# A two-layer graph attention kernel: sets of seven matrix products run into each other, the second product runs one graph later, and score rows are spread by GpSimd

## The chip, the cores and the metric

The kernel runs on one core of one Trainium2 chip. A core has five engines with their own instruction queues: TensorE (PE in the profile; its weight loads are listed apart as PEld), VectorE (DVE), ScalarE (ACT), GpSimd (POOL) and SyncE (SP, which here only issues transfers). TensorE writes to PSUM, which VectorE and ScalarE read. Sixteen DMA engines move data between HBM and the core's SBUF. The metric is the device time of one execution in microseconds (us).

## What is computed

The input is x of shape (32, 512, 512) in float32, that is 32 graphs of 512 nodes with 512 features, and a 0/1 matrix adj of shape (32, 512, 512) in int32. Each graph goes through a layer norm with ReLU, two layers of graph attention and a residual sum:

```python
def gat_layer(x, mask, W, a_src, a_dst, bias, concat):
    xl = (x @ W).reshape(B, N, H, F)
    asrc = jnp.einsum('bnhf,hf->bnh', xl, a_src)
    adst = jnp.einsum('bnhf,hf->bnh', xl, a_dst)
    e = jax.nn.leaky_relu(asrc[:, :, None, :] + adst[:, None, :, :], 0.2)
    e = jnp.where(mask[..., None], e, NEG_INF)
    attn = jax.nn.softmax(e, axis=1)
    out = jnp.einsum('bsdh,bshf->bdhf', attn, xl)
    ...
h = jnp.maximum(_layernorm(x, axis=-1), 0.0)
mask = (adj > 0) | jnp.eye(N, dtype=bool)[None]
h1 = jax.nn.elu(gat_layer(h, mask, W1, att_src1, att_dst1, b1, concat=True))
out = x + gat_layer(h1, mask, W2, att_src2, att_dst2, b2, concat=False)
```

The first layer has H = 4 heads of F = 256 features, the second one head of 512. So a graph needs four large products: x by W1 ("project1"), attention by features for four heads ("gather1"), h1 by W2 ("project2") and attention by features again ("gather2").

## The kernel before

**Products in sets of seven.** Each large product of 2 x 2 blocks is done with seven block products instead of eight (Strassen's scheme in Winograd's form). `sevens` (L866) does project1, project2 and gather2; `gather1` (L1079) does the heads' products in pairs. The sums of blocks that feed the seven products are VectorE subtractions (`sums` L823, `sums1` L1016, `sums2` L1225). Three running sums, named "a", "b" and "g" in `ACC` (L864), each hold one double bank of PSUM; product 1 is copied from a's bank to g's (the `COPY2` of `mm` into `mm` on ScalarE), and after each product its bank is emptied to SBUF by ScalarE (`act` with Copy) or VectorE (subtract or add). PSUM has four double banks, handed out by `Banks` (L45). `LAST` (L907) gives the order of the seven: 1, 5, 6, 3, 7, 2, 4; `PAIRS_OF` (L1070) gives 1, 5, 6, 2, 7, 3, 4 for gather1. Each set is run to its end before the next begins.

**Attention weights.** `Soft` (L657) makes the attention weights of one head. `columns` (L691) takes the node scores and spreads the row of source scores to all 128 partitions; `first` (L710) makes each target's maximum and sum over 128 x 512 blocks: leaky ReLU on ScalarE (`l<-as,z`), masked minimum on VectorE (`l<-l,mt`), exponential on ScalarE (`l<-l,low`). Its results form a row that is spread too (`rr`); `second` (L763) builds the weights `p` from that row: four VectorE sums (`p<-rr,z`), two transfers by GpSimd that add the mask from HBM to p (`accumulate`, L430, `p<-dm`), and four exponentials on ScalarE (`p<-p,z`). `spread` (L665) brings a row to all partitions: a VectorE transpose, a small transfer to HBM (`das`, `drr`), and a transfer that reads it back once for each partition (`as<-das`, `rr<-drr`, 512 KB).

**Other parts.** `masks` (L555) turns adj into a bf16 mask `m`, writes it to HBM (`dm`) and transposes it by DMA (`mt`). `norm` (L586) makes the layer norm's statistics, with the root as a power on GpSimd (L597); `norm_turn` (L606) normalises on ScalarE and turns x by a DMA transpose (`x<-adj`) between two ScalarE copies (`adj<-x`, `ht<-x`). `elu` (L983) finishes the first layer.

**What sets the order.** The program is not emitted as it is written. Every instruction is added to a `Program` (L87) with its engine, a planned cost and the keys it reads and writes. TensorE's order is the written one; for ScalarE, VectorE, GpSimd and SP a planner (`order`, L234) simulates the run from the planned costs and picks an order, which each engine then follows strictly. Transfers are planned with a fixed lead, a size and a tail (L97). The steady loop (L1371) handles at step i: gather1 of graph i+1 (two pairs), project1 of graph i+2 (two halves), the second layer's softmax and gather2 of graph i, and project2 of graph i+1.

Of the kernel before, what the change touches and what calls it, by code (L numbers as in the profile page):

```python
# [44 lines left out]
class Banks:  # L45


    def __init__(self, tiles):
        self.tiles = tiles
        self.free = [(i, j) for i in range(len(tiles)) for j in range(2)]  # L50
        self.written = {q: 512 for q in self.free}

    def take(self, width=512, seeded=0):
        n = [sum(i == k for k, _ in self.free) for i in range(len(self.tiles))]
        fit = [q for q in self.free if self.written[q] >= seeded]
        half = next((q for q in fit if n[q[0]] == 1), fit[0])
        least = min(self.written[q] for q in fit)
# [15 lines left out]
    def take2(self, width, seeded=0):  # L73
        whole = [i for i, j in self.free if j == 0 and (i, 1) in self.free]
        least = {i: min(self.written[i, j] for j in range(2)) for i in whole}
        i = min((i for i in whole if least[i] >= seeded), key=least.get)
        self.free = [q for q in self.free if q[0] != i]
        for j in range(2):
            self.written[i, j] = max(width, self.written[i, j] if seeded else 0)
        return [("mm", i, j) for j in range(2)], self.tiles[i]  # L80
# [218 lines left out]
def tile_gat(  # L299
# [66 lines left out]
    half = sbuf.tile([P, NT], F32, name="half")  # L366
    nc.vector.memset(half, -0.5)
# [11 lines left out]
    xl2 = sbuf.tile([P, NT, DO + 2], F32, name="xl2")  # L379
# [7 lines left out]
    xrs = slots("xr", 4, [P, N])  # L387
    ls = slots("l", 3, [P, N])
    ps_ = slots("p", 3, [P, NT, N])
    m = sbuf.tile([P, NT, N], BF16, name="m")  # L390
# [5 lines left out]
    drs = slots("drr", 2, [2 * NT, P], F32, dram)  # L396
    mds = slots("dm", 3, [P, NT, N], BF16, dram)
    stats = slots("stats", 2, [P, NT, nc.vector.BN_STATS_DIM + nc.vector.BN_AGGR_DIM + 1])
    zs = slots("z", 4, [P, 5, 2, NT])
# [13 lines left out]
    )  # L413

# [140 lines left out]
    def masks(b):  # L555

        for t in range(NT):
            ak, a = adjs.take()
            dma(0.75, (), [ak], a, adj[b, t * P : (t + 1) * P, :])
            dve(  # L560
                0.34, [ak], [("m", t)], nc.vector.tensor_scalar,
                m[:, t, :], a, 0.0, -BIG, op0=OP.is_le, op1=OP.mult,
            )
            adjs.give(ak)
        blocks = bass.AP(tensor=m.tensor, offset=m.offset, ap=[m.ap[0], [N + P, NT], [1, P]])
        every = [("m", t) for t in range(NT)]
        dve(
            0.5, every, every, nc.vector.tensor_max,
            blocks, blocks, diag[:, None, :].to_broadcast([P, NT, P]),
        )  # L570
        MASK[b] = mk, md = mds.take()
        dma(0.45, every, [mk], md.rearrange("p t n -> p (t n)"), m.rearrange("p t n -> p (t n)"))
        tk, mt = mts.take()

        for t in (0, 2):
            prog.add(
                "SP", 1.3, every, [tk + (t // 2,)],
                lambda t=t: nc.sync.dma_start_transpose(
                    mt[:, t : t + 2].rearrange("p t d r -> p (t d) r"),
                    m[:, t : t + 2].rearrange("p t n -> p (t n)"),  # L580
# [5 lines left out]
    def norm(b):  # L586
        sk, st = stats.take()
        S, A = nc.vector.BN_STATS_DIM, nc.vector.BN_AGGR_DIM
        for t, (xk, xt) in enumerate(XT[b]):
# [4 lines left out]
        dve(TINY, every, every, nc.vector.tensor_scalar_add, rstd, st[:, :, S + 1], EPS)  # L594
        prog.add(
            "POOL", 1.0, every, every,
            lambda: nc.gpsimd.tensor_tensor(rstd, rstd, half, op=OP.pow),  # L597
        )
# [58 lines left out]
    class Soft:  # L657
# [7 lines left out]
        def spread(self, v, keys, rows, to, through, n=NT):  # L665

            k = rows * n
            ok, o = to.take()
            dk, dr = through.take()

            c = 32 // k
            sb = o[:, 0, :32]
            dve(
                0.12, keys, [ok], nc.vector.transpose,
                sb, bass.AP(tensor=v.tensor, offset=v.offset, ap=[v.ap[0], [1, k], [0, c]]),
            )
            dma(
                0.03, [ok], [dk], dr[:k].rearrange("k (b j) -> b k j", j=32),
                bass.AP(
                    tensor=sb.tensor, offset=sb.offset, ap=[[c * sb.ap[0][0], P // c], [1, 32]]  # L680
                ),
                0.55,
            )
            dma(
                0.18 * rows * n, [dk], [ok], o[:, :rows, : n * P],
                bass.AP(tensor=dr.tensor, offset=dr.offset, ap=[[0, P], [n * P, rows], [1, n * P]]),
            )
            through.give(dk)
            return ok, o

        def columns(self, i, given=None):  # L691
# [15 lines left out]
                z[:, 0].rearrange("p h t -> p (h t)"), keys, n, ass, das  # L707
            )

        def first(self, h, parts=((0, NT),)):  # L710
# [9 lines left out]
            for d0, d1 in parts:  # L720
# [35 lines left out]
                self.rr[h].append((d0, d1, *self.spread(v, [wk + (2, d0)], 2, rrs, drs, n)))  # L756
# [6 lines left out]
        def second(self, h):  # L763
# [9 lines left out]
            for d0, d1, rk, rr in self.rr.pop(h):  # L773
                at, n, cs = slice(d0 * P, d1 * P), (d1 - d0) * P, range(d0 // 2, d1 // 2)
                long = n == N
                for u in range(NT):
# [7 lines left out]
                    if here:  # L784
                        dve(
                            0.59 if long else 0.34, keys + [("m", u)], keys, nc.vector.tensor_add,
                            p[:, u, at], p[:, u, at], m[:, u, at],
                        )
                rrs.give(rk)
                if not here:  # L790
                    mk, md = MASK[self.b]
                    for us in (0, 1), (2, 3):
                        keys = p_keys(pk, us)
                        accumulate(
                            2.2, keys + [mk], keys,
# [70 lines left out]
    def sevens(left, right, rkeys, put, kh, units, width, order, seeds={}):  # L866
# [3 lines left out]
        for us, n in order:  # L870
            acc, first = ACC[n], n in (1, 5) or n == 2 and us not in forked
            if first:
                seed = seeds.get(n)
                bank[us, acc] = banks.take2(width, 0 if seed is None else M)
# [19 lines left out]
            if n == 1 and banks.able(width):  # L894
                bank[us, "g"] = gks, gt = banks.take2(width, width)
# [11 lines left out]
    LAST = tuple(((0, 1), n) for n in (1, 5, 6, 3, 7, 2, 4))  # L907
    FOUR = LAST + tuple(((2, 3), n) for _, n in LAST)

    PARTS = tuple(((0, 1), n) for n in (1, 2, 5, 6, 3, 7, 4))  # L910
# [168 lines left out]
    def gather1(soft, order):  # L1079
# [11 lines left out]
        for u, n in order:  # L1091
# [3 lines left out]
            if n == 4:  # L1095
                for f in late:
                    f()
# [367 lines left out]
```

## Time and profile before

| | |
|---|---|
| median of 3 runs | 2851.67 us (2849.85 to 2853.57) |
| profiled execution | 2858.08 us, span of its instructions 2856.3 us |
| TensorE busy | 2770.0 us, mean granted clock 0.993 |
| VectorE busy | 2432.2 us |
| ScalarE busy | 2384.9 us |
| GpSimd busy | 322.6 us |
| DMA | 501.42 MB, 176 GB/s |

The profile lists instructions by the line of the helper that recorded them: L439 are all matmuls, L425 VectorE's, L422 ScalarE's, L433 the accumulating transfers, L428 the other transfers. So the names of the tiles tell which step an instruction belongs to: `h` is the first layer's output, `hs` and `t` hold block sums, `mm` is PSUM, `xl` holds features. A group's line gives its busy time and the mean length of one, then the idle time of its engine just before it and what ended that idle time. A float32 matmul appears as two records.

### The profile page before, as it was taken

The numbers are of one execution on the slowest core, as the hardware profiler recorded it, in microseconds if no ns is written. First come the engines' busy times: TensorE is split into PE (matmuls) and PEld (weight loads), VectorE is DVE, ScalarE is ACT, GpSimd is POOL, SyncE is SP. The second block draws the span as 40 slices with busy tenths as digits, with TensorE's granted clock in tenths as the row PEclk, the third lists the DMA queues.
The fourth block names the chain that finished last, engine by engine and source line by source line (L and its number), as shares of the span: only waits on it lengthen the run. The fifth ranks groups of instructions, "written<-read, shape, count | busy, mean of one in ns | idle before, by whom it ended". The sixth has DMA issues, their size and how long they took to land.

```text
span 2856.3 us, 39591 instructions
## 1 busy us (share of the span) xinstructions
PE 2770.0 (97%) x12520; PEld 2373.9 (83%) x12520; DVE 2432.2 (85%) x5494; ACT 2384.9 (83%) x4506; POOL 322.6 (11%) x356
## 2 busy tenths in 40 slices
PE   7999999999999999999999999999999999999988
PEld 6688888888888888888888888888878888888876
DVE  7888898888898878879889888888878988888885
ACT  5888898878898888878888888888878898888882
POOL 0111111101111101111011100111101111111110
PEclk9999999999999999999999999999999999999999
DMA  7666767666777667776687776777666767666652
GB/s 226 153 176 167 204 161 188 181 174 170 189 188 177 176 166 196 167 173 179 172 181 167 196 155 184 170 176 197 164 168 178 195 174 178 183 183 177 176 141 96
DMA packets 369077, 501.42 MB, mean 176 GB/s; under 512 B 220260, under 2 KB 225124, under 8 KB 368868
## 3 DMA queue, kind: packets, MB, share of 16 engines
q1 hardware_dynamic: 323076, 332.15, 42.5%
q0 software_dynamic: 45792, 166.74, 25.6%
q8 instruction: 100, 1.64, 0.2%
q14 instruction: 109, 0.89, 0.1%
HBM read 315.89 MB, written 51.31 MB: 129 GB/s over the span
## 4 chain that ended last, share of the span: by engine, by line
PE 79%; DMA 9%; ACT 5%; DVE 5%; issue 2%; SPq 0%; POOL 0%; ACTq 0%; POOLq 0%; DVEq 0%
PE mm L439 79%; DMA p<-dm 4%; DMA x<-adj 3%; DVE p L425 1%; ACT l L422 1%; ACT p L422 1%; DMA as<-das 1%; ACT adj L422 1%; ACT ht L422 1%; DVE l L425 1%; DVE t L425 1%; DVE hs L425 1%; DVE h L425 1%; ACT xl L422 0%; ACT xr L422 0%
## 5 line engine op out<-in xcount | busy, mean ns | idle before, releaser
L439 PE MATMUL mm<-w_sb,hs 128*128 128x257 f32 (+2 forms) x3032 | 685.3, 383 | 25.1 <-ACT h L422 16.1
L439 PEld LDWEIGHTS mm<-w_sb,hs 128*128 128x128 f32 x3032 | 576.1, 191 | 120.7 <-ACT h L422 20.1
L433 POOL DMA_DIRECT2D p<-dm x314 | 274.4, 878 | 2420.4 <-DVE p L425 1459.7
L422 ACT ACTIVATE l<-l,low 128x512 f32<-128x512 f32 x640 | 455.2, 713 | 40.0 <-DVE low L425 39.3
L439 PE MATMUL mm<-w_sb,ht 128*128 128x258 f32 x2112 | 482.6, 382 | 3.6 <-ACT ht L422 1.4
L425 DVE CUSTOM_DVE_ANT_1 l<-l,mt 128x512 f32<-128x512 f32 x640 | 425.2, 682 | 62.8 <-ACT l L422 62.2
L422 ACT ACTIVATE p<-p,z 128x512 f32<-128x512 f32 (+1 forms) x636 | 424.7, 709 | 62.3 <-DMA p<-dm 51.2
L439 PE MATMUL mm<-p,xl 128*128 128x256 f32 (+1 forms) x1984 | 470.6, 385 | 4.5 <-ACT h L422 3.0
L422 ACT ACTIVATE l<-as,z 128x512 f32<-128x512 f32 x640 | 436.9, 712 | 32.0 <-DMA as<-das 30.7
L439 PE MATMUL mm<-w_sb,h 128*128 128x257 f32 x2056 | 459.5, 380 | 3.3 <-DVE w_sb L425 3.3
L425 DVE SCALAR_TENSOR_TENSOR p<-rr,z 128x512 f32<-128x512 f32 (+1 forms) x636 | 448.1, 740 | 15.8 <-DMA rr<-drr 15.1
L439 PEld LDWEIGHTS mm<-w_sb,ht 128*128 128x128 f32 x2112 | 398.8, 190 | 67.6 <-ACT xl L422 3.3
L439 PEld LDWEIGHTS mm<-w_sb,h 128*128 128x128 f32 x2056 | 390.3, 190 | 62.3 <-DVE w_sb L425 3.7
L439 PEld LDWEIGHTS mm<-p,xl 128*128 128x128 f32 x1984 | 377.8, 191 | 68.0 <-issue 6.9
L422 ACT ACTIVATE xr<-h,b_sb 128x512 f32<-128x512 f32 x248 | 171.8, 714 | 120.9 <-DVE h L425 120.9
L422 ACT ACTIVATE xl<-mm 128x516 f32<-128x516 f32 (+2 forms) x376 | 218.4, 586 | 46.9 <-PE mm L439 45.6
L439 PE MATMUL mm<-t,hs 128*128 128x256 f32 x992 | 233.1, 386 | 25.0 <-ACT mm L422 22.0
L439 PEld LDWEIGHTS mm<-t,hs 128*128 128x128 f32 x992 | 189.7, 193 | 57.5 <-ACT mm L422 27.1
L425 DVE SCALAR_TENSOR_TENSOR h<-h,b_sb,xr 128x512 f32<-128x512 f32 x248 | 181.5, 744 | 46.5 <-ACT xr L422 46.4
L422 ACT ACTIVATE ht<-x 128x1024 uint16<-128x1024 uint16 x120 | 159.3, 1351 | 30.2 <-DMA x<-adj 30.2
L439 PE MATMUL mm<-xl,p 128*128 128x256 f32 (+1 forms) x752 | 180.2, 388 | 2.3 <-DVE t L425 1.6
L422 ACT ACTIVATE h<-mm 128x512 f32<-128x512 f32 (+1 forms) x256 | 146.3, 574 | 26.5 <-PE mm L439 24.4
(113 smaller groups left out, 3268.0 us busy)
## 6 DMA issues: line engine op xcount, KB each, us to landing
p<-dm POOLq DMA_DIRECT2D x314, 512.0 KB, 5.6
rr<-drr SPq DMA_DIRECT2D x159, 512.0 KB
x<-in_x_dram SPq DMA_DIRECT2D x128, 256.0 KB
adj<-in_adj_dram SPq DMA_DIRECT2D x128, 256.0 KB
as<-das SPq DMA_DIRECT2D x64, 512.0 KB
t<-in_x_dram SPq DMA_DIRECT2D x62, 512.0 KB
out_dram<-t SPq DMA_DIRECT2D x60, 512.0 KB
dm<-m SPq DMA_DIRECT2D x32, 512.0 KB
```

Of the source, the lines that this page charges most:

```text
L422: prog.add("ACT", cost, reads, writes, lambda: nc.scalar.activation(*a, **k))
L425: prog.add("DVE", cost, reads, writes, lambda: f(*a, **k))
L433: lambda: nc.gpsimd.dma_start(to, at, accum_op=OP.add), size,
L439: f(*a, **k)
```

## The change

Six things are changed together.

1. **Sets run into each other.** The order of the seven becomes 1, 5, 6, 2, 3, 7, 4 (`SEVEN`). A new helper `pipe` runs a set up to its sixth product; the seventh (product 4) of the set before is placed after the first two products of the new set. `whole` does the same around project2, which keeps the old order (`NEAR`), placing it after that set's first product. project1 is called for one half of the heads at a time. `Banks.take2` gives fixed banks by role: a alternates between banks 0 and 1, b has bank 2, g has bank 3. Two identity products at the start write bank 3 once.
2. **The second product runs one graph later.** At step i the loop runs `second` of the second layer and gather2 for graph i-1 instead of i.
3. **Two feature buffers** for the second layer (`xl2s`), and to make room: `xr` 4 to 2, `l` 3 to 2, the mask `m` from four to two row tiles.
4. **Rows to one partition by transfer, to the others by GpSimd.** `spread` is split. `lay` transposes and writes the row to HBM; `spread` reads it back into one partition and calls GpSimd's `partition_broadcast`. For the `rr` rows `spread` is now called in `second` instead of `first`.
5. **The mask in halves.** `masks` handles two row tiles at a time; each half has its own transfer to HBM and its own transpose. The last graph's mask is read back from HBM.
6. **The norm's root** is a logarithm and an exponential on ScalarE and four small VectorE instructions, instead of GpSimd's power. The last block sum of gather1 and gather2 (`late`) is made after product 2, in place.

```diff
+    ROLE = {"a": (0, 1), "b": (2,), "g": (3,)}
...
-    def take2(self, width, seeded=0):
-        whole = [i for i, j in self.free if j == 0 and (i, 1) in self.free]
-        least = {i: min(self.written[i, j] for j in range(2)) for i in whole}
-        i = min((i for i in whole if least[i] >= seeded), key=least.get)
+    def take2(self, role, width, seeded=0):
+        whole = [
+            i for i, j in self.free if j == 0 and (i, 1) in self.free
+            and min(self.written[i, q] for q in range(2)) >= seeded
+        ]
+        own = self.ROLE[role]
+        if role == "a":
+            own = (1 - self.last, self.last)
+        i = next((i for i in own if i in whole), None)
...
-    xl2 = sbuf.tile([P, NT, DO + 2], F32, name="xl2")
+    xl2s = tiles("xl2", 2, [P, NT, DO + 2])
...
-    xrs = slots("xr", 4, [P, N])
-    ls = slots("l", 3, [P, N])
+    xrs = slots("xr", 2, [P, N])
+    ls = slots("l", 2, [P, N])
...
-    m = sbuf.tile([P, NT, N], BF16, name="m")
+    m = sbuf.tile([P, 2, N], BF16, name="m")
+    flips = slots("flip", 4, [P, 32])
...
-        dve(TINY, every, every, nc.vector.tensor_scalar_add, rstd, st[:, :, S + 1], EPS)
-        prog.add(
-            "POOL", 1.0, every, every,
-            lambda: nc.gpsimd.tensor_tensor(rstd, rstd, half, op=OP.pow),
-        )
+        v, a = st[:, :, S + 1], st[:, :, 0]
+        dve(TINY, every, every, nc.vector.tensor_scalar_add, v, v, EPS)
+        act(0.25, every, every, rstd, v, AF.Ln)
+        act(0.25, every, every, rstd, rstd, AF.Exp, scale=-0.5)
+        dve(TINY, every, every, nc.vector.tensor_mul, a, rstd, rstd)
+        dve(TINY, every, every, nc.vector.tensor_mul, a, a, v)
+        dve(TINY, every, every, nc.vector.tensor_scalar, a, a, -0.5, 1.5, op0=OP.mult, op1=OP.add)
+        dve(TINY, every, every, nc.vector.tensor_mul, rstd, rstd, a)
...
+        def spread(self, laid, to):
+
+            dk, dr, rows, n, through = laid
+            ok, o = to.take()
+            k = rows * n
+            flat = bass.AP(tensor=o.tensor, offset=o.offset, ap=[o.ap[0], [1, k * P]])
             dma(
-                0.18 * rows * n, [dk], [ok], o[:, :rows, : n * P],
-                bass.AP(tensor=dr.tensor, offset=dr.offset, ap=[[0, P], [n * P, rows], [1, n * P]]),
+                0.03, [dk], [ok], flat[0:1],
+                bass.AP(tensor=dr.tensor, offset=dr.offset, ap=[[0, 1], [1, k * P]]),
+            )
+            prog.add(
+                "POOL", 0.25 + 1.2 * k / 8, [ok], [ok],
+                lambda: nc.gpsimd.partition_broadcast(flat, flat[0:1]),
             )
...
-    LAST = tuple(((0, 1), n) for n in (1, 5, 6, 3, 7, 2, 4))
-    FOUR = LAST + tuple(((2, 3), n) for _, n in LAST)
+    SEVEN = 1, 5, 6, 2, 3, 7, 4
+    LAST = tuple(((0, 1), n) for n in SEVEN)
+
+    NEAR = tuple(((0, 1), n) for n in (1, 5, 6, 3, 7, 2, 4))
...
+    def pipe(products):
+
+        for at in range(6):
+            if at == 2:
+                flush()
+            next(products)
+        behind.append(products)
+
+    def whole(products):
+
+        next(products)
+        flush()
+        run(products)
...
+    for i in range(B - 2):
         s = S1[i + 1]
+        pipe(gather1(s, PAIRS_OF[0]))
+        left1 = sums(ht_blocks(), KQ, 0.59)
+        pipe(project1(i + 2, left1, 0))
+        s.second(2)
+        s.second(3)
+        if i:
+            S2[i - 1].second(0)
+        S2[i] = second_layer(i)
+        masks(i + 2)
+        pipe(gather1(s, PAIRS_OF[1]))
+        n = S1[i + 2] = Soft(i + 2, 1, scores_1)
+        n.columns(0)
+        n.first(0)
+        n.first(1)
+        pipe(project1(i + 2, left1, 1))
+        n.second(0)
+        n.second(1)
+        if i:
+            residual(i - 1)
+            pipe(gather2(i - 1, S2[i - 1], sums2(i - 1, S2[i - 1])))
...
+        left2 = sums(h1_blocks(), KH, 1.15)
+        whole(project2(i + 1, left2, NEAR))
```

## Prediction

> **What bounds the kernel now.** I read the page's busy table first, then busy time by stage, then TensorE's waits in the middle of the run, then the timelines of TensorE and ScalarE around the longest of these.
>
> ```profile
> span 2856.3 us, 39591 instructions
> PE 2770.0 (97%) x12520; PEld 2373.9 (83%) x12520; DVE 2432.2 (85%) x5494; ACT 2384.9 (83%) x4506; POOL 322.6 (11%) x356
> ```
>
> TensorE is the bound; nothing in the change takes work from it (6276 matmuls before, 6278 after, each two records). So the only thing to win is time in which TensorE waits or runs at a lower clock. By stage (columns: stretch, length, then busy of PE, PEld, DVE, ACT, POOL with counts, granted clock, DMA share, GB/s):
>
> ```profile
> 0.00:150.00 150.00, 127.69 (x508) 96.61 (x509) 121.49 (x386) 104.14 (x202) 17.21 (x24) 0.98 0.72 190
> 150.00:2700.00 2550.00, 2503.10 (x11438) 2167.63 (x11437) 2204.46 (x4876) 2194.25 (x4121) 294.99 (x320) 1.00 0.70 178
> 2700.00:2856.30 156.30, 139.21 (x578) 109.61 (x576) 106.29 (x233) 86.50 (x184) 10.38 (x12) 0.97 0.43 122
> ...
> 360.00:450.00 90.00, 90.00 (x417) 78.55 (x416) 78.64 (x176) 79.94 (x151) 10.06 (x11) 1.00 0.66 173
> 2070.00:2160.00 90.00, 83.54 (x375) 71.85 (x374) 72.56 (x163) 71.81 (x137) 8.37 (x9) 0.96 0.68 170
> ```
>
> The middle holds 46.9 us of idle TensorE, the start 22.3 and the end 17.1. A stretch without a wait takes 417 matmul records in 90 us; the one at 2070 lost 42 of them, half by waiting and a part by a lower clock. Clock below 1.00 shows in five of the 90 us stretches of the middle (0.98, 0.98, 0.96, 0.98, 0.96): 90 x (3 x 0.02 + 2 x 0.04) = 12.6 us. So the middle can give back some 59 us at most, 2% of the time. What TensorE waits for there:
>
> ```profile
> PE mm L439 <- ACT mm L422: 22.5, 14, 5.4
> PE mm L439 <- ACT h L422: 18.0, 9, 5.6
> PE mm L439 <- DVE t L425: 2.0, 2, 1.2
> ```
>
> Nearly all is ScalarE emptying or copying a PSUM bank. Why is it late with an engine only 83% busy? The timelines of two of the worst:
>
> ```profile
> 2072.26 0.58 ACT L422 ACTIVATE h<-mm 128x512 f32<-128x512 f32 x1
> 2081.09 1.34 ACT L422 ACTIVATE ht<-x 128x1024 uint16<-128x1024 uint16 x1 [8.24 <-DMA x<-adj]
> 2082.30 0.69 ACT L422 ACTIVATE xr<-h,b_sb 128x512 f32<-128x512 f32 x1
> 2082.90 0.57 ACT L422 ACTIVATE h<-mm 128x512 f32<-128x512 f32 x1
> ...
> 2075.98 1.90 PE L439 MATMUL mm<-w_sb,ht 128*128 128x258 f32 x8
> 2083.53 7.23 PE L439 MATMUL mm<-w_sb,hs 128*128 128x258 f32 x24 [5.64 <-ACT h L422]
> ...
> 1714.71 1.33 ACT L422 ACTIVATE p<-p,z 128x512 f32<-128x512 f32 x2 [6.88 <-DMA p<-dm]
> 1718.08 0.58 ACT L422 ACTIVATE mm<-mm 128x512 f32<-128x512 f32 x1
> ...
> 1718.71 3.53 PE L439 MATMUL mm<-t,hs 128*128 128x256 f32 x8 [5.42 <-ACT mm L422]
> ```
>
> ScalarE stands in its fixed order behind a transfer that landed late, with the bank's eviction queued behind that. TensorE has one product of slack: 8 records, 8 x 0.216 = 1.73 us (90/417). At 2083 it is product 5 of a projection that needs the bank of the last set's product 4; at 1718 product 6 that needs product 1 copied off, with product 5 alone between.
>
> **What the Trainium skill says.** (1) "TensorE: Matmul & The Clock Gate", Part 1: an idle window of about 3.4 us halves the clock. The trace agrees in kind: the lowered stretches are those with waits of 2.7 to 5.6 us, so a long wait costs more than itself. (2) "DMA: Bandwidth & Descriptors", Issuing engines are not separate DMA queues: transfers of all engines share the same 16. Agrees: the transposes and p<-dm that ScalarE waits for run beside SP's row transfers at a share of 0.70. (3) "SBUF — State Buffer", Who interferes with whom: a VectorE instruction with two SBUF inputs and a GpSimd instruction that reads SBUF exclude each other. Half seen: GpSimd's power of four elements took 1036 ns with VectorE idle and 1404 in the median, and no VectorE instruction beside it was longer; a long GpSimd read is not in this trace. (4) "GPSIMD Engine Reference", 3.1 (Elementwise) and 2.1 (Instruction dispatch), give the prices used below.
>
> **The change part by part.**
>
> *Order and banks.* With 1,5,6,2,3,7,4, the last product put behind the next set's first two, and fixed roles for the four double banks, each reuse of a bank has two products or more ahead of it: one more than now, 1.73 us. The 39 idle stretches of the middle, read one by one from TensorE's timeline: 5.64, 5.42, 4.36, 3.68, 3.10, 2.68, 1.89, 1.83, 1.80, and thirty of 1.69 or less. Less 1.73 each, nine remain, of 14.8 in sum: 46.9 - 14.8 = **-32.1**. Bounds: the planner may fill the slack with other ScalarE work (a quarter, -12) or all of it may go (-47).
>
> *Clock.* What remains has three waits over 2.5 us instead of six: of 12.6 us I let 8 go: **-8** (-3 to -12.6).
>
> *Rows by GpSimd.* Removed from SP's transfers: 159 + 64 of 512 KB and 34 of 256 KB, 125.8 MB of q1's 332.15.
>
> ```profile
> q1 hardware_dynamic: 323076, 332.15, 42.5%
> rr<-drr SPq DMA_DIRECT2D x159, 512.0 KB
> as<-das SPq DMA_DIRECT2D x64, 512.0 KB
> ```
>
> By bytes that is 0.379 x 42.5% = 16% of the engines' time: DMA share from 0.68 to some 0.52. Transposes share SP's queue with these, so I expect the late landings to shorten; on the 14.8 us left, **-4** (0 to -10). The row itself: a 4 KB transfer and a broadcast replace a 512 KB one (das to as was 5 to 7 us in the chain). The trace has no broadcast. Below it is at least the fixed part, 1.0 us (the 1036 ns). Above, the skill's two-input 2.6 cycles an element at 1.2 GHz, 1024 elements, 2.2 us, with that fixed part and one VectorE instruction waited for (0.74): 4 us. I take 1.0 plus the page's 1.03 cycles (0.88 us): 1.9, an estimate. GpSimd then has 322.6 - 48.4 (the power) + 223 x 1.9 + 34 x 1.44 = 747 us, 27%: no bound. Queued behind a waiting broadcast are the p<-dm issues (0.88 us each), and behind these ScalarE's exponentials. They need that same row first, or another's; GpSimd idles 2420 us before them now, which hides it, and if that cover fails it is up to 2.5 us of landing per broadcast. The first call's load of about 6 us (same page, 2.1) falls where GpSimd waits for its first row.
>
> *VectorE and ScalarE.* The norm's root: 32 x 4 more VectorE instructions of 0.16 = 20.5 us; the mask in halves +4 (estimate from 32 of 0.41); ScalarE 64 x 0.195 = 12.5. Beside 85% and 83% with 15% idle: **+2** for TensorE. Port exclusion and the halved buffers (xr 4 to 2, l 3 to 2, m to two tiles, so that the second mask half waits for both transfers of the first on SP's queue): **+4** (0 to +50; a gain I exclude, since both only add waits).
>
> *Second product one graph later.* It moves with its row, 4 VectorE sums, 2 p<-dm, 4 exponentials, its 8 sums, two loads and two stores past one graph on SP and GpSimd; counts stay. It loosens the chain from scores to product by some 88 us (2856/32), already in the cut above. The last such softmax half falls into the end, where VectorE is 43.5 us busy in 50: 4 x 0.74, **+3** (-2 to +8). Splitting mask transfers adds 33 issues on SP of about 0.4 us, hidden by SP's waits (over 2000 us). Start: the two identity products run before the first norm ends: 0 (-3 to +3).
>
> Sum: -32.1 - 8 - 4 + 2 + 4 + 3 = -35.1. The profiled execution took 2858.1 (span 2856.3), 6.4 above the median of the runs, 2851.7; I take the difference off the median: **2816.6, say 2816**.
>
> **The rivals.**
>
> *A, all late waits go.* If fewer bytes also end the late landings, 46.9 + 12.6 go and 5 come: 2797. For it: both timelines end in a transfer. Against: some waits are on VectorE or plain order.
>
> *B, it does not do what it says.* The planner orders ScalarE by its own landing times, so a longer slack lets evictions stand behind more. A quarter of the waits goes, clock -3, additions +5: -11.7 - 3 + 5 = -9.7, 2842. For it: what is late is not what the planner counts on.
>
> *C, slower: VectorE is blocked at the shared port.* If each of 257 broadcasts holds VectorE for its read, 0.85 us: 2432 + 24 + 218 = 2674 us. The busiest 90 us without a wait now has VectorE at 81.3, 90%; it passes that at 2820 us of span from (0.90 x 2820 - 2456)/257 = 0.32 us per broadcast. At 93%, between the 90% seen and full, 2674/0.93 = 2875. For it: most VectorE instructions have two SBUF inputs. Against: GpSimd's power delayed none of them.
>
> **How the numbers follow.** Forecast 0.57 (2800 to 2835), A 0.14 (2785 to 2800), B 0.15 (2835 to 2850), C 0.14 (2850 up). Measurement tells 0.2%, 5.7 us: faster means under 2846. B leaves a third of itself within 0.2%: 0.05. Faster 0.57 + 0.14 + 0.10 = 0.81, same 0.05, slower 0.14. The range 2790 to 2856 leaves out some 0.05 of A and 0.11 of C.
>
> **What would show it.** TensorE's idle in the middle near 15 us, no "ACT h" among long waits, the waits for "ACT mm" fewer than 8; clock at 1.00 nearly throughout; DMA share near 0.52; GpSimd near 750 us; VectorE near 2456. Wrong if VectorE's idle names GpSimd, if TensorE's waits move to VectorE, or if ScalarE still waits 7 us for x<-adj and p<-dm with TensorE behind it.

## The result, and the profile after

| | before | after |
|---|---|---|
| median of 4 runs each, side by side on one chip | 2852.62 us (2849.85 to 2857.31) | 2881.02 us (2874.55 to 2885.98) |
| ratio, 95% interval | 1 | 1.0105 (1.0073 to 1.0137) |
| span of the profiled execution | 2856.3 us | 2878.5 us |
| TensorE idle: first 150 us, middle, after 2700 us | 22.3, 46.9, 17.1 us | 28.7, 56.6, 13.6 us |

The change made the kernel 1.05% slower; 1.25% faster was forecast. The idle times are each stage's length (up to the span's end) less TensorE's busy time in it. First the busy times on the page of the kernel after:

```profile
span 2878.5 us, 40547 instructions
PE 2779.6 (97%) x12524; PEld 2377.8 (83%) x12524; DVE 2591.8 (90%) x5653; ACT 2396.1 (83%) x4570; POOL 662.4 (23%) x581
```

ScalarE is near where it was. VectorE has risen by 159.6 us, of which 24 had been expected. TensorE has two matmuls more (four records, 0.9 us) and is busy 9.6 us longer. By stage, with the columns as in the prediction:

```profile
0.00:150.00 150.00, 121.28 (x451) 87.31 (x452) 119.39 (x378) 97.74 (x197) 25.34 (x28) 0.95 0.53 137
150.00:2700.00 2550.00, 2493.38 (x11371) 2157.17 (x11369) 2335.42 (x4990) 2192.77 (x4158) 605.92 (x524) 1.00 0.54 132
2700.00:2880.00 180.00, 164.91 (x704) 133.30 (x704) 137.01 (x287) 105.61 (x217) 31.17 (x29) 0.98 0.38 108
```

In the first 150 us TensorE ran 451 matmul records where it had run 508 (57 x 0.216 = 12 us behind), and in the middle 67 fewer again (14.5 us). That is the loss, spread over the whole run. The DMA share fell as forecast, to 0.54. What TensorE waits for in the middle (waiting engine and line, engine waited for; us in all, times, longest):

```profile
PE mm L457 <- DVE hs L443: 25.1, 23, 5.2
PE mm L457 <- ACT xl L440: 14.4, 17, 2.3
PE mm L457 <- ACT mm L440: 8.6, 5, 4.1
PE mm L457 <- DVE t L443: 4.4, 4, 2.2
...
PE mm L457 <- ACT h L440: 1.1, 1, 1.1
```

The old waits went as forecast: "ACT h" from 18.0 us in 9 to 1.1 in 1, "ACT mm" from 22.5 in 14 to 8.6 in 5. New ones have come: the block sums `hs` that VectorE makes, and the features `xl`. GpSimd's new instruction, from the page's groups (count, busy us, mean ns, then GpSimd's idle time before it):

```profile
L723 POOL PARTITION_BROADCAST rr<-rr x161 | 277.0, 1722 | 714.3 <-DMA rr<-drr 662.5
L723 POOL PARTITION_BROADCAST as<-as x96 | 139.9, 1457 | 690.1 <-DMA as<-das 534.7
```

Now the timeline where one of the `hs` waits ended (start, duration, instruction, idle time before it):

```profile
336.90 1.39 POOL L723 PARTITION_BROADCAST rr<-rr  x1
337.15 1.45 DVE L443 TENSOR_TENSOR p<-p,t 128x512 f32<-128x512 f32 x1
...
339.14 1.30 POOL L723 PARTITION_BROADCAST rr<-rr  x1 [0.85 <-DMA rr<-drr]
339.46 1.38 DVE L443 TENSOR_TENSOR hs<-ht 128x512 f32<-128x512 f32 x1
...
340.77 0.68 DVE L443 TENSOR_TENSOR hs<-xl,hs 128x512 f32<-128x512 f32 x1
...
340.90 2.52 PE L457 MATMUL mm<-w_sb,hs 128*128 128x258 f32 x5 [2.52 <-DVE hs L443]
```

A sum of 128x512 takes 0.68 us where nothing is beside it, as the third one here. The first two take 1.45 and 1.38, each beginning beside a broadcast, and TensorE, which has been waiting for 2.52 us, starts 0.06 us after the second of them ends. The two together are 1.5 us longer than they would be. TensorE's order is the same in the experiments that keep the order, so the same matmul can be found there by counting: it waits 0 with rows by transfer and 0.11 us where GpSimd writes zeros instead. The longest wait of all, 5.2 us for `hs` at 212 us, is a poorer witness, for it lasts 3.6 us with rows by transfer too.

Over all of VectorE's instructions in the trace, 238 are more than 60 ns above the median of their shape, by 167 us together; 158 of them overlap an `rr` broadcast (118 us) and 79 an `as` broadcast (49 us); the longest delay is 1.21 us. In the trace of the kernel before it is 8 instructions and 0.5 us.

Of the prediction's signs of being wrong, TensorE's waits did move to VectorE. The other, VectorE's idle time with GpSimd's name on it, shows nothing: the holding lies inside the instructions, as busy time. The weights' sums, which read the rows that GpSimd makes, have on the page

```profile
L443 DVE SCALAR_TENSOR_TENSOR p<-rr,z 128x512 f32<-128x512 f32 (+1 forms) x636 | 467.8, 770 | 1.3 <-PE mm L457 1.3
```

that is 1.3 us of idle time ahead of 636 of them, none of it put down to GpSimd, and 770 ns for one (0.74 us where nothing is beside it).

### The profile page after: what moved, and what is told of

Its sections match the earlier page's. It is cut to its first block, busy times and chain, and to the rows that moved or that the text cites. A ratio compares the mean times of both kernels' runs of the same rounds, so it can differ in the third digit from the quotient of the medians.

```text
span 2878.5 us, 40547 instructions
## 1 busy us (share of the span) xinstructions
PE 2779.6 (97%) x12524; PEld 2377.8 (83%) x12524; DVE 2591.8 (90%) x5653; ACT 2396.1 (83%) x4570; POOL 662.4 (23%) x581
## 5 line engine op out<-in xcount | busy, mean ns | idle before, releaser
L457 PE MATMUL mm<-w_sb,hs 128*128 128x257 f32 (+2 forms) x3032 | 704.1, 383 | 28.3 <-DVE hs L443 26.1
L443 DVE CUSTOM_DVE_ANT_1 l<-l,mt 128x512 f32<-128x512 f32 x640 | 434.6, 698 | 84.4 <-ACT l L440 80.6
L457 PE MATMUL mm<-w_sb,ht 128*128 128x258 f32 x2112 | 502.6, 382 | 7.4 <-DVE xl L443 4.7
L457 PE MATMUL mm<-p,xl 128*128 128x256 f32 (+1 forms) x1984 | 481.3, 385 | 7.3 <-ACT p L440 4.5
L440 ACT ACTIVATE l<-as,z 128x512 f32<-128x512 f32 x640 | 434.8, 711 | 49.4 <-POOL as L723 48.5
L443 DVE SCALAR_TENSOR_TENSOR p<-rr,z 128x512 f32<-128x512 f32 (+1 forms) x636 | 467.8, 770 | 1.3 <-PE mm L457 1.3
L723 POOL PARTITION_BROADCAST rr<-rr x161 | 277.0, 1722 | 714.3 <-DMA rr<-drr 662.5
L723 POOL PARTITION_BROADCAST as<-as x96 | 139.9, 1457 | 690.1 <-DMA as<-das 534.7
L440 ACT ACTIVATE xl<-mm 128x514 f32<-128x514 f32 (+2 forms) x380 | 222.6, 586 | 72.8 <-PE mm L457 71.9
L457 PE MATMUL mm<-xl,p 128*128 128x256 f32 (+1 forms) x1024 | 250.0, 386 | 6.9 <-DVE t L443 4.9
L457 PEld LDWEIGHTS mm<-xl,p 128*128 128x128 f32 x1024 | 193.1, 189 | 43.7 <-DVE t L443 7.5
```

Source lines behind the costliest of these rows:

```text
L440: prog.add("ACT", cost, reads, writes, lambda: nc.scalar.activation(*a, **k))
L443: prog.add("DVE", cost, reads, writes, lambda: f(*a, **k))
L457: f(*a, **k)
L723: lambda: nc.gpsimd.partition_broadcast(flat, flat[0:1]),
```

## The experiments

My theory after the result was that the broadcast, which reads SBUF, holds VectorE, and that the rest of the change is worth what was forecast. The rivals: the sets run into each other are themselves the loss; the rows come later through GpSimd than by transfer; the planner's new order for ScalarE, VectorE and SP is worse. The runs below took place in four groups on four chips. The kernel before had medians of 2836.33, 2854.22, 2843.44 and 2840.86 us in them, so ratios are to the kernel before on the same chip, and times in us are compared within a group. The ratios are those on record; the quotients of the medians lie within their intervals. Between groups a ratio can be off by more than its interval: two kernels below that have nearly the same time, 2806.49 and 2802.45 us, have ratios of 0.9878 and 0.982.

**Rows by transfer, in the order of after.** GpSimd's instruction is left out while its planned slot stays, so that every engine keeps the order of the kernel after.

```diff
-                0.03, [dk], [ok], flat[0:1],
-                bass.AP(tensor=dr.tensor, offset=dr.offset, ap=[[0, 1], [1, k * P]]),
...
-                lambda: nc.gpsimd.partition_broadcast(flat, flat[0:1]),
...
+                0.03, [dk], [ok], flat,
+                bass.AP(tensor=dr.tensor, offset=dr.offset, ap=[[0, P], [1, k * P]]),
+            )
+            prog.add("POOL", 0.25 + 1.2 * k / 8, [ok], [ok], lambda: None)
```

> The changed kernel with one thing undone: each row is again read back by one 512 KB transfer to all partitions, and GpSimd's broadcast is gone. The order on TensorE, VectorE, ScalarE and SP is that of the changed kernel. T1 (broadcasts block VectorE at the shared port, and that is the loss): VectorE busy falls from 2592 to about 2430 us and the time to 2825 to 2840. T2 (the new order, the shrunk buffers or the later second product cost the time, and VectorE's longer instructions lie in its idle time): VectorE falls as well, the time stays at 2870 to 2885. T3 (the start alone is slower): the time stays within 10 us of 2881 and the first 150 us stay short of work by some 57 matmul records.

Measured: 2817.35 us, ratio 0.9916 (0.9887 to 0.9944). Its busy line:

```profile
PE 2755.0 (98%) x12524; PEld 2373.0 (84%) x12524; DVE 2445.1 (87%) x5653; ACT 2391.7 (85%) x4570; POOL 277.3 (10%) x324
```

With the same 5653 instructions in the same order VectorE is busy 2445.1 us instead of 2591.8: 147 us less for 257 broadcasts, 0.57 us each (0.65 by the count of lengthened instructions). TensorE idles 16.9 us in the middle instead of 56.6. The order is not the loss. The time is below the 2825 to 2840 us expected for this theory.

**No broadcast and no heavy transfer.** The 4 KB transfer stays and the broadcast is left out; the row tiles are set to zero once, so softmax is made from zeros on 127 partitions.

```diff
-                lambda: nc.gpsimd.partition_broadcast(flat, flat[0:1]),
...
+            prog.add("POOL", 0.25 + 1.2 * k / 8, [ok], [ok], lambda: None)
...
+        for rows in (*ass.tiles, *rrs.tiles):
+            nc.gpsimd.memset(rows, 0.0)
```

> The changed kernel without its broadcasts: the rows go to one partition only, the other partitions hold zeros written at the start, so the attention weights are not the reference's. Neither the 512 KB transfers nor the broadcasts run; all else is in the same order. It shows what the rest of the change is worth. T1: 2805 to 2830, VectorE near 2430. T2: 2865 to 2880. Against the run with rows by transfer it shows the worth of the lighter transfers: 4 to 10 us faster if they matter, equal if not.

Measured: 2806.49 us, ratio 0.9878 (0.9838 to 0.9918); VectorE 2444.4 us, middle idle 8.0 us, DMA share 0.54. The lighter transfers alone, against the run above, are worth 11 us in medians whose runs lie 2814 to 2818 and 2798 to 2812. With the kernel after this gives the broadcast's price: 1.0105/0.9878 = 1.023, some 65 us (75 by the medians of the two groups).

**The broadcast twice.**

```diff
-                lambda: nc.gpsimd.partition_broadcast(flat, flat[0:1]),
+                lambda: [nc.gpsimd.partition_broadcast(flat, flat[0:1]) for _ in range(2)],
```

> The changed kernel with every broadcast done twice in a row, the second writing the same values. T1: VectorE grows by up to 165 us again, to about 2750, and the time by at least as much as the first dose cost, to 2930 to 2990. T2: VectorE grows, the time stays under 2895. If the second broadcast of a pair falls on an idle VectorE more often, the growth is smaller than the first dose's, but in T1 never under 20 us.

Measured: 3072.18 us, ratio 1.0822 (1.0787 to 1.0857). Its busy line, and below it TensorE's waits in the middle:

```profile
PE 2844.8 (93%) x12524; PEld 2400.7 (78%) x12524; DVE 2757.9 (90%) x5653; ACT 2399.2 (78%) x4570; POOL 1032.1 (34%) x838
```

```profile
PE mm L457 <- DVE hs L443: 62.3, 23, 5.1
PE mm L457 <- ACT xl L440: 50.2, 36, 3.8
```

The same two waits as in the kernel after, grown from 25.1 and 14.4 us. VectorE is held 337 us in 458 instructions: twice the broadcasts, twice the holding, but several times the loss, and well above the 2930 to 2990 us expected. (A second broadcast also makes every row come later; more on this below.) VectorE's share stays at 90%, because the span grows with it.

**Rows by transfer, planned as such.** The transfer of the first edit with a planned size of `0.18 * k` for its 512 KB, and no entry for GpSimd at all, so that the planner makes its own order.

> As the run with rows by 512 KB transfers, but the planner is told of the transfer's size as in the kernel before and GpSimd's entries are gone, so the order of ScalarE, VectorE and SP is planned for it. T1: 2815 to 2835, at or below the run with the kept order, and faster than the kernel before. T2: 2865 or more.

Measured: 2806.67 us (2802.23 to 2814.01), ratio 0.9883 (0.985 to 0.9915). Its stages:

```profile
0.00:150.00 150.00, 129.20 (x497) 94.97 (x498) 120.56 (x396) 105.71 (x208) 11.72 (x19) 0.95 0.67 189
150.00:2700.00 2550.00, 2538.39 (x11669) 2212.65 (x11669) 2261.08 (x5128) 2245.71 (x4268) 259.67 (x301) 1.00 0.69 181
2700.00:2800.00 100.00, 88.45 (x360) 66.71 (x359) 63.01 (x130) 45.06 (x95) 4.75 (x6) 1.00 0.41 119
```

Against the stages of the kernel before: 11669 records in the middle instead of 11438, at the same DMA share (0.69 and 0.70) and with VectorE busier (2261 and 2204 us). TensorE's idle time is 20.8, 11.6 and 12.0 us. The change without its fourth part is faster than both kernels.

**The broadcast put into the kernel before.**

```diff
-                0.18 * rows * n, [dk], [ok], o[:, :rows, : n * P],
...
+                0.03, [dk], [ok], flat[0:1],
...
+            prog.add(
+                "POOL", 0.25 + 1.2 * k / 8, [ok], [ok],
+                lambda: nc.gpsimd.partition_broadcast(flat, flat[0:1]),
+            )
```

> The kernel before with one part of the change: its 257 rows go to one partition by transfer and to the others by GpSimd's broadcast; sets, buffers, masks and the norm's root stay as before. T1 (the shared port): VectorE grows by some 150 us to about 2580 and the time by 25 to 80 us over the kernel before. T2 (only the new order, in which VectorE's work is packed more tightly, suffers): time within 10 us of before, whatever VectorE shows.

Measured: 3159.45 us, ratio 1.1072 (1.1045 to 1.1098), far more than either theory had. Three of this kernel's waits over the whole run, each behind the one above it:

```profile
POOL stats L597 <- issue: 217.2, 29, 8.2
...
DVE stats L425 <- POOL stats L597: 175.7, 30, 7.4
...
PE mm L439 <- DVE xl L425: 164.1, 30, 11.4
```

and the timeline of GpSimd at one of them:

```profile
1283.79 1.29 POOL L691 PARTITION_BROADCAST rr<-rr  x1
1292.12 1.05 POOL L597 TENSOR_TENSOR stats<-stats,half 128x4 f32<-128x4 f32 x1 [7.04 <-issue]
```

GpSimd stands for 7.04 us ahead of the norm's power with nothing to wait for, VectorE waits for the power, TensorE for VectorE. The trace has 124 instructions that load a GpSimd library; the kernel before has 2, the kernel after 4. So broadcast and power seem to lie in different libraries, with a load at each change. The Trainium skill, "GPSIMD Engine Reference", 2.1 (Instruction dispatch), gives about 6 us for the first call to a freshly loaded kernel; here a wait of that kind stands ahead of 29 of the 32 powers, at a mean of 217.2/29 = 7.5 us, and ahead of broadcasts another 117.5 us in 22 waits. The sixth part of the change, the root without GpSimd, is what keeps this out of the kernel after. To see the broadcast alone I moved the root too, with the sixth part's `norm` put into this kernel:

> The kernel before with the 257 broadcasts and with the norm's root on ScalarE and VectorE as in the change, so that GpSimd runs one library only. L1 (the 305 us were mostly the switching of libraries, some 7 us at each of 32 powers and again behind them, with VectorE and ScalarE waiting for the norm): 2870 to 2930, VectorE about 2580. L2 (the old order, without slack, suffers that much from the shared port): 3050 or more.

Measured: 2895.18 us, ratio 1.0177 (1.0144 to 1.0209); VectorE 2576.4 us, 227 instructions lengthened by 154 us, TensorE idle 68.4 us in the middle. Broadcast in place of heavy transfers, with the root moved, costs the old arrangement 1.8%; in the new one, against the run with rows by transfer in the same order, it is 1.0105/0.9916 = 1.019. It is slow by itself, wherever the sets stand.

**Sets one by one.** On the version with rows by transfer, each set is run to its end, in its new order.

```diff
     def pipe(products):
-        for at in range(6):
-            if at == 2:
-                flush()
-            next(products)
-        behind.append(products)
+        run(products)
```

> The planned kernel with rows by 512 KB transfer, but each set of seven runs to its end before the next begins; the order 1, 5, 6, 2, 3, 7, 4, the banks by role and the later second product stay. S1 (the gain comes from the sets running into each other): 12 to 25 us slower than the version with rows by transfer, with TensorE's waits for ScalarE's evictions back at set borders. S2 (it comes from the second product one graph later and the order within a set): within 6 us of it.

Measured: 3007.02 us, ratio 1.0529 (1.05 to 1.0559). TensorE's waits in the middle:

```profile
PE mm L457 <- DVE h L443: 65.7, 56, 6.8
PE mm L457 <- DVE xl L443: 55.5, 56, 2.3
PE mm L457 <- DVE t L443: 25.1, 27, 1.4
```

That is some 200 us above the version with rows by transfer, where at most 25 had been expected, but it doesn't test the overlap alone: in the order 1, 5, 6, 2, 3, 7, 4 product 4 comes straight behind 7, whose bank VectorE must empty first (56 times `h`, 56 times `xl`). The order makes sense only with the overlap. So a second try also used orders with a product between 7 and 4: the old ones for project1 (`NEAR`) and gather1, and gather1's 1, 5, 6, 2, 7, 3, 4 for gather2 too, which had 1, 5, 6, 3, 7, 2, 4 before:

> The planned version with rows by 512 KB transfer and the second product one graph later, but every set runs to its end and the sets have orders with a product between 7 and 4 (1, 5, 6, 3, 7, 2, 4 for the first projection, 1, 5, 6, 2, 7, 3, 4 for both attention products); banks by role stay. The earlier run of sets one by one had product 4 straight behind 7 in the same bank, which made 1 us of wait in each set. If that was its cost: 2825 to 2860 here, the difference to 2807 being what running into each other is worth. If fixed banks without the overlap are at fault: 2900 or more.

Measured: 2838.35 us, ratio 0.9982 (0.9969 to 0.9994), middle idle 34.3 us, of which "ACT mm" is 18.6 us in 9 waits. And the other way round, the sets run into each other but the second product in its old place (only the last three graphs keep the later one):

```diff
-            S2[i - 1].second(0)
...
+        if i < B - 3:
+            S2[i].second(0)
...
-            pipe(gather2(i - 1, S2[i - 1], sums2(i - 1, S2[i - 1])))
+            pipe(gather2(i, S2[i], sums2(i, S2[i])))
```

> The planned version with rows by 512 KB transfer, but the second layer's weights and product stay with their own graph, as in the kernel before; sets run into each other as in the change. S1 (the gain comes from the sets): within 6 us of 2807. S2 (it comes from the later second product): 2825 to 2850, with TensorE waiting for ScalarE's p or VectorE's hs.

Measured: 2842.36 us, ratio 0.9998 (0.9983 to 1.0013), middle idle 29.5 us. TensorE's largest waits there:

```profile
PE mm L457 <- ACT p L440: 11.4, 13, 3.2
PE mm L457 <- DVE hs L443: 10.8, 13, 4.4
```

Without the later product TensorE waits for the weights `p` and for block sums; without the overlap it waits for ScalarE's work on the banks. With the rest of the change in place, either half alone leaves some 30 us of idle time and a time near that of the kernel before; together they leave 11.6 us and 0.9883. Each of these two runs alone would have passed for the proof of one cause; only both show that neither half works without the other.

**GpSimd writes and does not read.** The broadcast is replaced by setting the same tile to zero (softmax is made from zeros).

```diff
-                lambda: nc.gpsimd.partition_broadcast(flat, flat[0:1]),
...
+            prog.add("POOL", 0.25 + 1.2 * k / 8, [ok], [ok], lambda: nc.gpsimd.memset(flat, 0.0))
```

> The changed kernel with each broadcast replaced by a GpSimd memset of the same 128 partitions and the same length, so that GpSimd writes as much but reads nothing; the attention weights are not the reference's, as the rows are zeros. Order as in the changed kernel. If the read is what excludes VectorE: VectorE busy within 25 us of 2444 and the time within 8 us of the run without broadcasts. If the write excludes it too: VectorE 2500 or more and the time 20 us or more above the run without broadcasts.

Measured: 2802.45 us, ratio 0.982 (0.9799 to 0.984). Its page:

```profile
PE 2756.0 (98%) x12524; PEld 2375.8 (85%) x12524; DVE 2454.7 (88%) x5653; ACT 2398.3 (86%) x4570; POOL 505.4 (18%) x581
...
L721 POOL MEMSET rr<- 128x1024 f32 (+1 forms) x161 | 172.7, 1072 | 754.1 <-DMA rr<-drr 754.1
```

The same 581 instructions on GpSimd at the same places and in the same order, 1.07 us long, and VectorE is busy 10 us longer than with nothing there (2444.4), where the broadcast adds 147. Some holding shows (63 instructions, 38 us, counted as before); it costs no time that can be seen. By kind of instruction the difference is plain. Of VectorE's instructions with two tensor inputs (`TENSOR_TENSOR`, `SCALAR_TENSOR_TENSOR`) 583 overlap a broadcast in the kernel after and 183 of them are lengthened; here 530 overlap GpSimd's writes and 9 are. Of `TENSOR_SCALAR`, with one tensor, it is 28 of 52 there and 41 of 53 here; of the stream transposes and the norm's statistics none in either. So GpSimd's being busy is not what holds the two-input instructions that make up most of the loss. That it is the reading fits this, and the rule on reads and writes that the prediction names; it isn't shown by itself, for the zeros are also a different instruction, and shorter.

Nor do late rows explain the loss of the kernel after: here too the readers stand behind an instruction of GpSimd that follows the same transfer. VectorE had not waited for rows in the kernel after, and ScalarE, whose leaky ReLU reads the `as` rows, waited no longer for GpSimd there (48.5 us) than for the transfers in the first experiment (54.3 us).

**Which rows?** `as` rows by broadcast and `rr` rows by transfer; the reverse; and `as` rows by two broadcasts each; all in the order of the kernel after.

```diff
+            n_p = P if to is rrs else 1
-                0.03, [dk], [ok], flat[0:1],
+                0.03, [dk], [ok], flat[0:n_p],
...
-                lambda: nc.gpsimd.partition_broadcast(flat, flat[0:1]),
+                lambda: None if n_p > 1 else nc.gpsimd.partition_broadcast(flat, flat[0:1]),
```

> The changed kernel with the broadcast for the 96 source-score rows alone; the 161 rows of the second kind come by 512 KB transfer. Order as in the changed kernel. If cost goes with the number of broadcasts: VectorE +55 to +65 us over 2445, and the time about 37% of the way from the run with all rows by transfer (0.992 of before) to the changed kernel (1.0105): 0.999 of before. If TensorE is touched only past some 90% of VectorE: 0.991 to 0.995.

> The changed kernel with the broadcast for the 161 rows of the second kind alone; the 96 source-score rows come by 512 KB transfer. Order as in the changed kernel. Only the source-score rows: VectorE 2487 us, time as with all rows by transfer (some 2815). Place (the second kind stands just ahead of the sums that fill p, and VectorE is full there): VectorE about 2550, time 2855 to 2880, nearly the changed kernel's. Load (only VectorE's total counts, from some 88% up): VectorE about 2550, time 2830 to 2855.

> As the run with the broadcast for the 96 source-score rows alone, but each done twice: 192 broadcasts. Order as in the changed kernel. Place: VectorE near 2530, time still within 8 us of 2815, since these rows stand where VectorE has room. Load: VectorE near 2530 and the time 2825 to 2845, on one line with the run of the other 161.

Measured, sorted by the time that VectorE is held (the first and the last two rows are from runs above):

| broadcasts | VectorE held, us | VectorE busy, us | TensorE idle in the middle, us | ratio |
|---|---|---|---|---|
| none, rows by transfer | 0.4 | 2445.1 | 16.9 | 0.9916 (0.9887 to 0.9944) |
| `as` | 49 | 2487.0 | 17.2 | 0.9865 (0.9836 to 0.9893) |
| `as` twice | 100 | 2534.6 | 37.4 | 1.0044 (1.0024 to 1.0065) |
| `rr` | 121 | 2550.9 | 44.3 | 1.0057 (1.0035 to 1.0079) |
| both (after) | 167 | 2591.8 | 56.6 | 1.0105 (1.0073 to 1.0137) |
| both twice | 337 | 2757.9 | 166.3 | 1.0822 (1.0787 to 1.0857) |

`as` alone came in below both ranges stated for it, `as` twice above both, and only `rr` alone fell in one, that for the place. So neither VectorE's load alone nor the place alone gives these numbers. The 49 us of `as` cost nothing that shows; the 121 us of `rr` bring 27 us more idle time of TensorE than rows by transfer. The rows with doubled broadcasts have a rival in them, since there each row also comes later. ScalarE's reading of the `as` rows (idle time before it at the end of the line) with `as` once, `as` twice and both twice:

```profile
L440 ACT ACTIVATE l<-as,z 128x512 f32<-128x512 f32 x640 | 435.0, 712 | 40.9 <-POOL as L724 39.7
L440 ACT ACTIVATE l<-as,z 128x512 f32<-128x512 f32 x640 | 435.5, 712 | 115.7 <-POOL as L724 114.7
L440 ACT ACTIVATE l<-as,z 128x512 f32<-128x512 f32 x640 | 434.8, 711 | 125.8 <-POOL as L723 125.0
```

How much of those two rows' cost is the holding and how much ScalarE's later start is open. With `rr` alone TensorE's largest wait is

```profile
PE mm L457 <- DVE hs L443: 26.8, 22, 5.1
```

nearly that of the kernel after (25.1 in 23): the `rr` broadcasts delay the block sums. The other wait, for the features `xl`, doesn't come apart in this way: 1.4 us in 2 times with `as`, 5.3 in 7 with `rr`, 14.4 in 17 with both. With `as` twice it is

```profile
PE mm L457 <- ACT xl L440: 15.5, 17, 2.4
```

**A planner that knows of it.** To the kernel after, VectorE's entry of 0.65 us that does nothing is added beside each broadcast, so that the planner counts the holding when it makes the order.

```diff
+            prog.add("DVE", 0.65, [ok], [ok], lambda: None)
```

> The changed kernel, all rows by GpSimd, with 0.65 us on VectorE planned behind each broadcast in which VectorE has nothing to do; so the planner counts the time that the broadcast holds it. If ignorance of the planner made the loss: 2815 to 2845. If it is VectorE's fill itself: within 12 us of 2881.

Measured: 2849.06 us, ratio 1.0016 (1.0001 to 1.003). VectorE is held as before (231 instructions, 166 us; 2595.4 us busy), but TensorE idles 34.9 us in the middle instead of 56.6. That is just outside the 2815 to 2845 us expected if ignorance of the planner made the loss. From 0.9883 to 1.0105 it is 2.2%: 0.9 of that went with the new order, and 1.3 is left (ratios from three chips). The entry does two things, though. It fills VectorE in the plan, and it plans the row's readers 0.65 us later; ScalarE's waits for `as` rows from GpSimd fell from 48.5 to 0.2 us. Which of the two brought the 0.9 is not separated. Last, `as` rows by broadcast and `rr` by transfer, both planned as what they are, since 49 us had cost nothing:

> Source-score rows by GpSimd, the others by 512 KB transfer, planned for both. If 96 broadcasts cost nothing and lighter transfers help: 2795 to 2806. If the 49 us on VectorE cost as much as the lighter transfers bring: 2804 to 2815, equal to the planned version with all rows by transfer.

Measured: 2822.45 us, ratio 0.9947 (0.9924 to 0.997). Slower than both ranges (2795 to 2815), and no better than all rows by transfer, 0.9883. That one stays the best of those that compute the whole.

## Why the prediction was wrong, step by step

**The step that failed** is "Port exclusion and the halved buffers [...]: +4 (0 to +50)". Rows by transfer in the same order give 0.9916 and no rows 0.9878, with the halved buffers still in, so those cost nothing that can be seen, and the loss comes with the broadcasts: 1.023 x, some 65 us, where +4 had been put down and 50 was the top of the bounds. The mechanism had been named as rival C, and the sum's other terms came out near enough together. What was wrong was the size of the term, and with it the chance of 0.14. The argument against C was that GpSimd's power had delayed no VectorE instruction. That reading of the trace was right: 31 of the 32 powers overlap VectorE's work, 76 two-input instructions in all, and none is longer by more than 64 ns. But the power reads four elements for each partition, a broadcast a whole row; that this is why it delayed none is likely and not tested. The prediction had also seen that the power itself grew beside VectorE, from 1036 to 1404 ns, and did not count that as a sign. The Trainium skill, "SBUF — State Buffer", Who interferes with whom, states that a VectorE instruction with two SBUF inputs contends with a GpSimd instruction that reads, and not with one that only writes. The counts above agree for the broadcast (183 of 583) and nearly so for the zeros (9 of 530). It makes no exception for a small read, so for the power the measurement decides. The page also lists copies and one-input `tensor_scalar` among those that can take the shared pair of ports; here too a 128x4 copy beside a broadcast took 0.66 us, against a median of 0.17:

```profile
2519.57 4.12 POOL L723 PARTITION_BROADCAST rr<-rr  x1
...
2523.05 0.66 DVE L443 COPY z<-xl 128x4 f32<-128x4 f32 x1
```

**Rival C's own numbers.** It had 0.85 us per broadcast, VectorE at 2674 us and a time of 2875. Measured: 0.57 to 0.65, 2591.8 and 2881. It came close by luck, because two errors cancel: the holding was a third to a half too large, and VectorE at 93% was too full; TensorE is delayed with VectorE at 90%. Its point of decision, 0.32 us per broadcast or 82 us in all, lies between the 49 us that cost nothing and the 121 us of `rr` broadcasts that did.

**Order and banks, -32.1; second product one graph later, "already in the cut above".** Right together: without the broadcast the middle's idle time falls from 46.9 to 11.6 us, -35.3. But the prediction read all of it off the slack of the banks and took the later product as a condition met. Apart, each is worth nothing or next to it (0.9998 and 0.9982), so the sum was right partly by luck.

**Clock, -8.** Right for the change without its broadcasts. The trace records the clock at half for 23.9 us of the middle before and 6.8 with rows by transfer as planned; at half the clock that is 12.0 and 3.4 us lost, -8.5. In the kernel after it is 23.9 again. The link to single long waits is looser than the prediction has it: in that run with rows by transfer drops followed waits of 1.96 and 2.54 us, shorter than the 3.4 us that it names, and in the kernel before a wait of 3.68 us at 242 us had none.

**Rows by GpSimd, -4.** Share 0.54 (0.52 forecast), broadcast 1.72 and 1.46 us (1.9), GpSimd 662 us (747). Lighter transfers were worth 11 us in the pair of runs with one order, and nothing against the version planned for heavy ones (2806.49 and 2806.67). Within its bounds or just out.

**VectorE and ScalarE, +2.** VectorE's added work is 12.5 us (2444.7 less 2432.2), half of the 24 forecast. The time of that version leaves little room for a larger cost.

**Start, 0 (-3 to +3).** Wrong where the broadcast is: 57 records behind. Without it the start is 11 to 44 records behind in seven runs (497 to 464 of 508), 2 to 10 us. I tried nothing on the start alone, so which part of the change costs this is open.

**End, +3.** TensorE's idle time in the last 150 us of the span fell from 17.1 to 13.6 us, 12.0 with rows by transfer as planned. No cost of the second softmax there shows.

Without its fourth part the change has a ratio of 0.9883; 2816 was forecast, 0.9875 of the median shown. So close an agreement is in part chance: the two traces come from different chips, and their spans differ by 55.8 us, more than the medians of one chip do (29.7).

**Open.** Which VectorE instruction meets which broadcast depends on landing times, so the same order can lose more or less. That 49 us cost nothing in the order of the kernel after (0.9865, 2814.52 us), and left 0.9947 (2822.45 us) in the planner's own, is not explained; part of it may be the two chips.

## What to carry to other kernels

Moving work to an idle GpSimd was not free here, where the work reads SBUF and VectorE is full of two-input instructions: count each such instruction as busy time of VectorE too (here 0.57 to 0.65 us for one that takes 1.3 to 1.7), in the sum and in any planner, and ask whether VectorE has room for it. An engine at 87% that feeds the bound can be harmless and at 90% not, but the share alone doesn't decide: with the planner told, VectorE was at 91% and TensorE idled less. Ask whether its last instruction ahead of a matmul can come late. A short instruction that showed no interference is weak evidence for a long one: look for one that reads as much, or give the rival the larger chance.

## What the runs showed of the hardware that was not expected

- VectorE's instructions beside a GpSimd broadcast of 1024 floats for each partition (512 for some) were longer by up to 1.21 us, 167 us in 238 instructions; beside a GpSimd write of the same tile (1.07 us) they were longer by 38 us in 63, most of them `TENSOR_SCALAR`, and VectorE's busy time rose by 10 us.
- A GpSimd power after a broadcast stood for some 7 us before it began (217.2 us in 29 times): mixing the two, with 124 library loads in the trace, made the kernel before 10.7% slower, where the broadcast with the root moved made it 1.8% slower.
- The broadcast took 1.29 us in the shortest case quoted here and 1.72 (`rr`) or 1.46 (`as`) in the mean, which mixes rows of 1024 and 512; beside VectorE it is recorded as up to 4.12 us in the line above.
